# One edge tile in 75 fetched row by row on ScalarE's queue, in the three edge passes of a graph network

## The chip, the cores and the metric

The kernel runs on one core of a Trainium2 chip. A core has a TensorE for matrix products (PE in the profile, its weight loads PEld), VectorE (DVE), ScalarE (ACT), GpSimd (POOL) and SyncE (SP), each with its own queue of instructions, and 16 DMA engines that they share. SP and ACT can issue DMAs at plain or computed addresses; POOL issues the indirect DMAs, whose row numbers lie in a tile. The metric is the device time of one execution in microseconds; before the change it is 34,256.46 us, the median of 10 runs (34,220.72 to 34,300.81).

## The reference

There are 30,000 nodes with 128 features and 960,000 edges, sorted by destination. Layer 0 normalises, applies relu, and runs two relational convolutions over the edges:

```
W   = einsum('rb,bdf->rdf', coeff, basis)        # 32 relations from 8 bases
Hr  = einsum('nd,rdf->nrf', h, W)
agg = segment_sum(Hr[src, etype] * norm, dst)    # + bias
```

Layer 1 is gated. For each of four edge types t it makes tables k, q and v of the nodes, and sums over the edges of type t

```
eta = sigmoid(k[dst] + q[src]);  msg = eta * v[src];  agg = segment_sum(msg, dst)
```

and adds `x @ Ws[t] + b[t]`; the four results are averaged. Both layers are added to x.

## The kernel before

The edges are cut into 7500 tiles of 128 (`TP`), three tiles make a group (`G`), five groups a block (`S`), five blocks a stage (75 tiles, `NTS`, 25 groups, `NGS`), four stages one turn of a hardware loop, and 25 turns a pass. There are three passes over all edges: two of the body in `rel_body` (the convolutions, tables `h0` and `h1`), and one of `gate_body` (table `qvtab`, 256 numbers a row). A turn is written out in full, in order, by hand (`manual_schedule`); an engine executes its own part of that order.

For each tile, `gather` (L117) has POOL issue an indirect DMA that brings 128 rows of the source nodes into SBUF, one edge a partition. In `rel_body`, VectorE makes for each tile a matrix `sb` (L476) from the edge's place in a window of 32 destinations and its coefficients; TensorE multiplies gathered rows and `sb` into the bank `pa` (L481), the three tiles of a group added together; ScalarE copies `pa` into `ab` (L485); and once a block TensorE multiplies `ab` with the bases (`bases_out`, L437). VectorE adds the finished windows to `agg`, which lies in SBUF (L374). The gathered tiles `hg` have 5 buffers, one a group, `sb` has 12, `pa` has 3. In the first pass SyncE loads edge types (`types`, `er`, L397), VectorE makes one-hot rows of them (L405), TensorE turns these into coefficients (L410), and those of the second pass are stored by ScalarE's queue (`keep`, L430) and loaded again in the second pass (`kept`, L435).

In `gate_body`, SyncE loads for each group 128 rows of the key table (`window`, `kw`, L521, 10 buffers, five groups ahead), at an address from a register; TensorE spreads them over the edges into `pk` (L538, 4 banks); VectorE adds the gathered q part of `qv` (L579); ScalarE takes the sigmoid in place (L580); two groups later VectorE multiplies with the v part (L547) and TensorE sums into windows (L549). `qv` has 10 buffers.

Beside the edge work, steps on the nodes are spread over the groups (`beside`): after the first pass's sums the hidden rows `h1`, in the second pass the tables `ktab` and `qvtab` (L655 to L709), in the third the output. Their stores go on ScalarE's queue. Stage loads (`idx` or `qi`, `relc`, `firsts`, `nrm`) go on SyncE's queue a stage ahead. The first destinations of a stage's groups are loaded into registers (`bases`, L360) on VectorE and, in the third pass, SyncE. The compiled program gives the DMAs of SP and ACT eight completion semaphores in turn; a DMA waits until the one eight before it in program order has landed.

Of the kernel before, what the change touches and what calls it, by code (L numbers as in the profile page):

```python
# [9 lines left out]
F32 = mybir.dt.float32  # L10
I32 = mybir.dt.int32
# [10 lines left out]
N = 30000  # L22
# [8 lines left out]
TP = 128  # L31
NT = E // TP
G = 3
# [3 lines left out]
S = 5  # L37
SB = 5
NQ = 4
NS = NQ * SB  # L40
NGS = S * SB
NTS = NGS * G
# [8 lines left out]
LEAD = 3 * VB  # L51
GAP = 8
EPS = 1e-5
CH = 5
PX, KX = 120, 10
IN_RANGE = "destinations are node numbers, below N"


def rows_of(col, n):
# [13 lines left out]
def kernel(  # L73
# [29 lines left out]
    nc = tc.nc  # L103
# [7 lines left out]
    qvtab = nc.dram_tensor("qvtab", (NX * T, 2 * D), F32, kind="Internal").ap()  # L111
    reld = nc.dram_tensor("reld", (TP, NT), F32, kind="Internal").ap()
    kcode = nc.dram_tensor("kcode", (E,), BF16, kind="Internal").ap()
    qidx = nc.dram_tensor("qidx", (TP, NT), I32, kind="Internal").ap()
    ce2 = nc.dram_tensor("ce2", (NI * NS, TP, S * G * B), F32, kind="Internal").ap()

    def gather(to, table, idx):  # L117
        nc.gpsimd.indirect_dma_start(  # L118
            out=to, out_offset=None, in_=table,
            in_offset=bass.IndirectOffsetOnAxis(ap=idx, axis=0))  # L120
# [23 lines left out]
    eps = consts.tile([P, 1], F32, name="eps")  # L144
    nc.vector.memset(eps, EPS)

# [37 lines left out]
    flag = consts.tile([1, 1], I32, name="flag")  # L184
    CT, CG = NT // CH, NGR // CH
    STEPS = N // (PX * KX)
    with tc.tile_pool(name="prep", bufs=2) as prep, tc.tile_pool(name="pre", bufs=4) as pre, \
            tc.tile_pool(name="prep_ps", bufs=1, space=PSUM) as prep_ps:
        lo = prep.tile([TP, CH], F32, name="lo", bufs=1)
        hi = prep.tile([TP, CH], F32, name="hi", bufs=1)  # L190

# [37 lines left out]

        for c in range(CH):  # L230
            edge_chunk(c)
            for i in range(c * STEPS // CH, (c + 1) * STEPS // CH):
                node_chunk(i)
        bad = prep.tile([TP, 2, CH], F32, name="bad", bufs=1)
        nc.vector.tensor_scalar(bad[:, 0, :], lo, 0.0, None, op0=ALU.is_lt)
# [60 lines left out]
    def sorted_path():  # L296
# [5 lines left out]
        with ExitStack() as all_:  # L302
# [57 lines left out]
            def bases(t, engine):  # L360
                _, vals = nc.values_load_multi_w_load_instructions(
                    t[:, :NGS], engines=[engine],
                    min_val=0, max_val=N - 1, skip_runtime_bounds_check_because=IN_RANGE)
                return vals

            def edge_row(row, i, s, n):

                return bass.AP(tensor=row.tensor, offset=(i * NG + s * S) * GE,
                               ap=[[0, n], [GE, S], [1, GE]])
# [6 lines left out]
            def rel_body(table, weights, second):  # L376
# [4 lines left out]

                def body(bas, i, io, pool, ps, cp, iw, ic, beside):
                    stage = {}
                    er, oh, pc, ce, ce_next, ab, po, base = {}, {}, {}, {}, {}, {}, {}, {}

                    def loads(k):
                        stage[k] = [stage_tile(io, "idx", src, I32, i, k),
                                    stage_tile(io, "relc", reld, F32, i, k),
                                    firsts(io, i, k)]
                        if not second:  # L390
                            stage[k].append(
                                stage_tile(io, "nrm", norm, F32, i, k, 4 * TQ - S * G))
# [62 lines left out]
                    for s in range(NS):  # L455
                        k = s // SB
                        if s % SB == 0:
                            if s:
                                tc.stage_boundary()
                            if k + 1 < NQ:  # L460
                                loads(k + 1)
                        if s % SB == 2:
                            leave_stage()
                        idx, relc, start = stage[k][:3]
                        if s + 2 < NS:
                            (kept if second else types)(s + 2)
                        ab[s] = pool.tile([P, B, S, W], F32, name="ab")
                        for g in range(S):
                            t0 = (s % SB * S + g) * G
                            hg = pool.tile([TP, G, D], F32, name="hg", bufs=5)  # L470
                            for j in range(G):
                                gather(hg[:, j, :], table, idx[:, t0 + j:t0 + j + 1])
                            pa = ps.tile([P, B, W], F32, name="pa", bufs=3)
                            for j in range(G):
                                sb = pool.tile([TP, B, W], F32, name="sb", bufs=12)
                                nc.vector.scalar_tensor_tensor(  # L476
                                    sb, iw[:TP].unsqueeze(1).to_broadcast([TP, B, W]),
                                    relc[:, t0 + j:t0 + j + 1],
                                    ce[s][:, g * G + j, :].unsqueeze(2).to_broadcast([TP, B, W]),
                                    op0=ALU.is_equal, op1=ALU.mult)  # L480
                                nc.tensor.matmul(pa.rearrange("p b w -> p (b w)"),  # L481
                                                 lhsT=hg[:, j, :],
                                                 rhs=sb.rearrange("p b w -> p (b w)"),
                                                 start=(j == 0), stop=(j == G - 1))
                            nc.scalar.copy(ab[s][:, :, g, :], pa)  # L485
                            if g == 1 and s:
                                bases_out(s - 1)
                            if g == 2 and not second and s + 1 < NS:
                                coefficients(s + 1)
                            if g == 3 and not second:  # L490
                                keep(s)
                                if s + 2 < NS:
                                    onehot(s + 2)
                            if g == 3 and s > 1:
                                add_windows(po[s - 2], base[(s - 2) // SB], s - 2)
                            if g == 3 and s % SB == 1:
                                base[k] = bases(start, DVE)
                            beside(s * S + g)
# [4 lines left out]

            def gate_body(i, io, pool, ps, cp, iw, ic, beside):
                stage = {}
                kb, oh, kw, sel, pk, qv, po, base, kbase = {}, {}, {}, {}, {}, {}, {}, {}, {}

                def loads(k):
                    stage[k] = [firsts(io, i, k)] + [stage_tile(io, *a, i, k) for a in (
# [25 lines left out]
                def keys(n):  # L535
                    pk[n] = ps.tile([TP, G, D], F32, name="pk", bufs=4)
                    for j in range(G):
                        nc.tensor.matmul(pk[n][:, j, :],  # L538
                                         lhsT=oh[n // S][:, n % S, j * TP:(j + 1) * TP],
                                         rhs=kw[n], start=True, stop=True)  # L540

                def sums(n):
                    s, g = n // S, n % S
                    if g == 0:
                        po[s] = ps.tile([P, S, W], F32, name="po")
                    msg = pool.tile([TP, G, D], F32, name="msg", bufs=3)
                    nc.vector.tensor_mul(msg, pk[n], qv[n][:, :, 1, :])  # L547
                    for j in range(G):
                        nc.tensor.matmul(po[s][:, g, :], lhsT=msg[:, j, :],  # L549
                                         rhs=sel[s][:, g * G + j, :],  # L550
                                         start=(j == 0), stop=(j == G - 1))
# [7 lines left out]
                for n in range(NG):  # L559
                    s, g, k = n // S, n % S, n // NGS  # L560
                    if n % NGS == 0:
                        if n:
                            tc.stage_boundary()
                        if k + 1 < NQ:
                            loads(k + 1)
                    if g == 0 and s % SB == 2:
                        leave_stage()
                    if g == 0 and s + 1 < NS:
                        types(s + 1)
                    if n + S < NG:  # L570
                        window(n + S)
                    qv[n] = pool.tile([TP, G, 2, D], F32, name="qv", bufs=10)
                    t0 = n % NGS * G
                    for j in range(G):
                        gather(qv[n][:, j].rearrange("p a f -> p (a f)"), qvtab,
                               stage[k][1][:, t0 + j:t0 + j + 1])
                    if n + 1 < NG:
                        keys(n + 1)
                    nc.vector.tensor_add(pk[n], pk[n], qv[n][:, :, 0, :])  # L579
                    nc.scalar.activation(pk[n], pk[n], AF.Sigmoid)  # L580
                    if n > 1:
                        sums(n - 2)
                    if g == 1 and s + 1 < NS:
                        onehot(s + 1)
                    if g == 4 and s:
                        add_windows(po[s - 1], base[(s - 1) // SB], s - 1)
                    if g == 4 and s % SB == 0:
                        base[k] = bases(stage[k][0], DVE)
                    beside(n)
# [347 lines left out]
    with tc.If(n_bad == 0) as cmp:  # L937
        sorted_path()
# [63 lines left out]
```

## Time and profile before

| what | value |
|---|---|
| median of 10 runs | 34,256.46 us |
| profiled execution's own time, its span | 34,293.53 us, 34,291.8 us |
| mean granted TensorE clock | 0.677 of full speed |
| busy: PE, PEld, DVE, ACT, POOL | 58%, 49%, 36%, 11%, 62% |
| indirect gathers (L118) | 15,000 of `hg` at 946 ns, 7500 of `qv` at 945 ns |
| gathers of `hg`, of `qv`, first and last start | 196.6 to 22,577.1 us; 22,621.6 to 34,259.3 us |
| DMA queue of POOL (q0) | 840,000 packets, 1967.52 MB |
| DMA queues of SP (q1) and ACT (q10) | 923,347 and 406,197 packets |

The durations are of one profiled execution, whose own time lies within the range of the ten runs. Instructions on registers and semaphores and those that issue DMAs are not counted as busy; a line such as "SPq" or "ACTq" is of such an instruction. In a line of groups, the number behind the bar is the busy time and the mean of one in ns, and behind the second bar stands the engine's idle time just before them and what ended most of it: the instruction that released it, "issue" where the profile shows no wait, "remote" where it knows no releaser. In the timeline each line has its start, its length, engine, line, operation and count, and in brackets the idle time ahead of it. In a list by line or tile the three numbers are the shortest, the median and the longest duration in ns.

### The profile page before, as it was taken

The page shows a single profiled execution, that of the slowest core. Times are in us where ns is not written, and L with a number is a line of the kernel's source. Part 1 is how long each engine was busy: PE and PEld are TensorE (multiplying, and loading weights), DVE is VectorE, ACT ScalarE, POOL GpSimd, SP SyncE. Part 2 cuts the span into 40 slices and gives each one's busy share as a digit, 9 for nine tenths or more (in the row PEclk, how much of TensorE's full clock was granted, in tenths as well). Part 3 has the DMA queues.
Part 4 walks back from the last instruction along what each step waited for, and adds up shares of the span by engine and source line. Part 5 has one row for each costly group of instructions (what it writes and reads, how often), then busy time and mean ns, then how long its engine had stood idle before and what let it go on. Part 6 is the DMA issues. An engine that isn't in the chain of part 4 may idle for free.

```text
span 34291.8 us, 321519 instructions
## 1 busy us (share of the span) xinstructions
PE 19888.5 (58%) x83304; PEld 16933.1 (49%) x83304; DVE 12372.1 (36%) x32695; ACT 3634.5 (11%) x9834; POOL 21303.1 (62%) x22514
## 2 busy tenths in 40 slices
PE   4555555555555566666666666655555555555555
PEld 3444444444444444444444444445555555555555
DVE  3333333333333333333333333333333333333333
ACT  1000000000000011111111111111111111111111
POOL 5666666666666666666666666656666666666665
PEclk8777777777777777777777777765555555555555
DMA  3222222222222222222222222234444444444444
GB/s 98 63 64 63 64 64 64 63 63 63 64 63 63 65 65 66 65 66 65 66 65 66 66 65 66 66 103 123 123 123 121 121 123 124 121 122 122 122 124 118
DMA packets 2171202, 2914.97 MB, mean 85 GB/s; under 512 B 684764, under 2 KB 1617880, under 8 KB 2169544
## 3 DMA queue, kind: packets, MB, share of 16 engines
q0 software_dynamic: 840000, 1967.52, 21.5%
q1 hardware_dynamic: 923347, 651.19, 6.6%
q10 hardware_dynamic: 406197, 276.11, 2.8%
q8 instruction: 802, 13.14, 0.2%
q14 instruction: 856, 7.01, 0.1%
HBM read 2618.79 MB, written 274.16 MB: 84 GB/s over the span
## 4 chain that ended last, share of the span: by engine, by line


## 5 line engine op out<-in xcount | busy, mean ns | idle before, releaser
L118 POOL DMA_INDIRECT hg<-h,idx x15000 | 14187.7, 946 | 8362.6 <-issue 4341.2
L481 PE MATMUL pa<-sb,hg 128*128 128x256 f32 x30000 | 9225.5, 465 | 6161.8 <-issue 3308.5
L481 PEld LDWEIGHTS pa<-sb,hg 128*128 128x128 f32 x30000 | 6900.0, 239 | 7986.1 <-issue 3838.4
L118 POOL DMA_INDIRECT qv<-qvtab,qi x7500 | 7088.4, 945 | 4593.7 <-issue 2256.8
L476 DVE SCALAR_TENSOR_TENSOR sb<-cp,relc,ce 128x256 f32<-128x256 f32 x15000 | 6129.1, 475 | 5245.0 <-remote 4012.1
L549 PE MATMUL po<-sel,msg 128*128 128x32 f32 x15000 | 3450.6, 386 | 4638.6 <-DVE msg L547 3265.6
L549 PEld LDWEIGHTS po<-sel,msg 128*128 128x128 f32 x15000 | 3406.8, 326 | 4937.1 <-DVE msg L547 3443.6
L538 PE MATMUL pk<-kw,oh 128*128 128x128 f32 x15000 | 3956.0, 437 | 307.1 <-DVE oh L525 271.0
L579 DVE TENSOR_TENSOR pk<-pk,qv 128x384 f32<-128x384 f32 x2500 | 1407.2, 563 | 7010.5 <-remote 5459.5
L485 ACT COPY ab<-pa 128x256 f32<-128x256 f32 x5000 | 1807.3, 373 | 19970.0 <-remote 10210.2
L538 PEld LDWEIGHTS pk<-kw,oh 128*128 128x128 f32 x15000 | 3452.1, 330 | 309.8 <-issue 309.8
L440 PE MATMUL po<-ab,bas 128*128 128x160 f32 x16000 | 2483.2, 311 | 371.4 <-ACT ab L485 215.2
L440 PEld LDWEIGHTS po<-ab,bas 128*128 128x128 f32 x16000 | 2406.7, 199 | 480.3 <-ACT ab L485 243.1
L374 DVE TENSOR_TENSOR agg<-agg,po 128x32 f32 x7500 | 1401.9, 187 | 2827.7 <-remote 704.3
L580 ACT ACTIVATE pk<-pk 128x384 f32<-128x384 f32 x2500 | 1186.0, 475 | 9316.8 <-DVE pk L579 5765.0
L676 PE MATMUL bank<-wall,hT 128*120 128x512 f32 x1524 | 1033.9, 801 | 937.7 <-issue 305.0
L547 DVE TENSOR_TENSOR msg<-pk,qv 128x384 f32<-128x384 f32 x2500 | 1368.3, 548 | 108.0 <-remote 95.8
L410 PE MATMUL cp<-coeff,oh 128*128 128x64 f32 x4000 | 689.2, 307 | 937.1 <-issue 800.4
L410 PEld LDWEIGHTS cp<-coeff,oh 128*128 128x128 f32 x4000 | 681.8, 232 | 1003.6 <-issue 905.6
L525 DVE TENSOR_TENSOR oh<-kb,cp 128x1920 f32<-128x1920 bf16 x500 | 1072.4, 2145 | 47.1 <-issue 31.8
L687 DVE TENSOR_TENSOR kt<-bank,ball 120x512 f32<-120x512 f32 x254 | 175.7, 692 | 2211.8 <-remote 788.0
L676 PEld LDWEIGHTS bank<-wall,hT 128*120 128x120 f32 x1524 | 344.4, 244 | 1269.8 <-issue 661.3
(77 smaller groups left out, 3383.1 us busy)
## 6 DMA issues: line engine op xcount, KB each, us to landing
hg<-h,idx POOLq DMA_INDIRECT x15000
kb<-kcode SPq DMA_DIRECT2D x500, 480.0 KB
kw<-ktab SPq DMA_DIRECT2D x2500, 64.0 KB
er<-in_et_row SPq DMA_DIRECT2D x2000, 64.0 KB
qvtab<-qvt ACTq DMA_DIRECT2D x254, 480.0 KB
qv<-qvtab,qi POOLq DMA_INDIRECT x7500
ktab<-kt ACTq DMA_DIRECT2D x254, 240.0 KB
ce<-ce ACTq DMA_DIRECT2D x500, 60.0 KB
```

Of the source, the lines that this page charges most:

```text
L118: nc.gpsimd.indirect_dma_start(out=to, out_offset=None, in_=table, in_offset=bass.IndirectOffsetOnAxis(ap=idx, axis=0))
L374: nc.vector.tensor_add(to, to, po[:, g, :])
L410: nc.tensor.matmul(pc[s][:, c].rearrange("p q l b -> p (q l b)"), lhsT=oh[s][:, c, :], rhs=coeff.rearrange("p q l b -> p (q l b)"), start= ...
L440: nc.tensor.matmul(po[s].rearrange("p s w -> p (s w)"), lhsT=bas[:, b, :], rhs=ab[s][:, b].rearrange("p s w -> p (s w)"), start=(b == 0), ...
L476: nc.vector.scalar_tensor_tensor(sb, iw[:TP].unsqueeze(1).to_broadcast([TP, B, W]), relc[:, t0 + j:t0 + j + 1], ce[s][:, g * G + j, :].uns ...
L481: nc.tensor.matmul(pa.rearrange("p b w -> p (b w)"), lhsT=hg[:, j, :], rhs=sb.rearrange("p b w -> p (b w)"), start=(j == 0), stop=(j == G ...
L485: nc.scalar.copy(ab[s][:, :, g, :], pa)
L538: nc.tensor.matmul(pk[n][:, j, :], lhsT=oh[n // S][:, n % S, j * TP:(j + 1) * TP], rhs=kw[n], start=True, stop=True)
L547: nc.vector.tensor_mul(msg, pk[n], qv[n][:, :, 1, :])
L549: nc.tensor.matmul(po[s][:, g, :], lhsT=msg[:, j, :], rhs=sel[s][:, g * G + j, :], start=(j == 0), stop=(j == G - 1))
L579: nc.vector.tensor_add(pk[n], pk[n], qv[n][:, :, 0, :])
L676: nc.tensor.matmul(bank(a, VB, T * D), lhsT=hT, rhs=wall[:, a].rearrange("p t f -> p (t f)"), start=True, stop=True)
```

## The change

The last tile of each stage is no longer gathered by POOL. Its 128 rows come into a tile of their own, `hx`, by 128 DMAs of one row each on ScalarE's queue. For that the stage's first group loads the tile's 128 row numbers into one partition (`ix`, on SyncE's queue), and after the copy of each of the first 21 groups (in the third pass: after each sigmoid) ScalarE issues the next 6 or 7 rows; ahead of every 16 it loads 16 numbers into registers. The product that used the last part of `hg` uses `hx`. In the third pass VectorE's addition and multiplication are split for a stage's last group, two tiles of `qv` and one of `hx`. This holds for all three passes.

```diff
+XR = 16
+NGX = NGS - 4
...
+            def last_tile(io, pool, table, array, i, k):
+                ix = io.tile([1, TP], I32, name="ix")
+                nc.sync.dma_start(
+                    ix, array[:, ds(i * (NQ * NTS) + (k + 1) * NTS - 1, 1)].rearrange("p o -> o p"))
+                to = pool.tile([TP, table.shape[1]], F32, name="hx")
+                vals = []
+
+                def fetch(n):
+                    for p in range(n * TP // NGX, min((n + 1) * TP // NGX, TP)):
+                        if p % XR == 0:
+                            _, vals[:] = nc.values_load_multi_w_load_instructions(
+                                ix[:, p:p + XR], engines=[mybir.EngineType.Activation], min_val=0,
+                                max_val=table.shape[0] - 1,
+                                skip_runtime_bounds_check_because=IN_RANGE)
+                        nc.scalar.dma_start(to[p:p + 1, :], table[ds(vals[p % XR], 1), :])
+
+                return to, fetch
...
                             hg = pool.tile([TP, G, D], F32, name="hg", bufs=5)
+                            rows = [hg[:, j, :] for j in range(G)]
+                            if t0 == 0:
+                                last[k] = last_tile(io, pool, table, src, i, k)
+                            if t0 + G == NTS:
+                                rows[-1] = last[k][0]
                             for j in range(G):
-                                gather(hg[:, j, :], table, idx[:, t0 + j:t0 + j + 1])
+                                if t0 + j + 1 < NTS:
+                                    gather(rows[j], table, idx[:, t0 + j:t0 + j + 1])
...
-                                                 lhsT=hg[:, j, :],
+                                                 lhsT=rows[j],
...
                             nc.scalar.copy(ab[s][:, :, g, :], pa)
+                            last[k][1](s % SB * S + g)
...
+                def parts(n):
+
+                    if n % NGS + 1 < NGS:
+                        return [(slice(0, G), qv[n])]
+                    hx = last[n // NGS][0].rearrange("p (o a f) -> p o a f", o=1, a=2)
+                    return [(slice(0, G - 1), qv[n][:, :G - 1]), (slice(G - 1, G), hx)]
...
-                    nc.vector.tensor_mul(msg, pk[n], qv[n][:, :, 1, :])
+                    for js, rows in parts(n):
+                        nc.vector.tensor_mul(msg[:, js], pk[n][:, js], rows[:, :, 1, :])
...
+                    if t0 == 0:
+                        last[k] = last_tile(io, pool, qvtab, qidx, i, k)
                     for j in range(G):
-                        gather(qv[n][:, j].rearrange("p a f -> p (a f)"), qvtab,
-                               stage[k][1][:, t0 + j:t0 + j + 1])
+                        if t0 + j + 1 < NTS:
+                            gather(qv[n][:, j].rearrange("p a f -> p (a f)"), qvtab,
+                                   stage[k][1][:, t0 + j:t0 + j + 1])
...
-                    nc.vector.tensor_add(pk[n], pk[n], qv[n][:, :, 0, :])
+                    for js, rows in parts(n):
+                        nc.vector.tensor_add(pk[n][:, js], pk[n][:, js], rows[:, :, 0, :])
                     nc.scalar.activation(pk[n], pk[n], AF.Sigmoid)
+                    last[k][1](n % NGS)
```

More of the change, by code (lines that the diff above doesn't have):

```diff
@@ L53 @@
 EPS = 1e-5
+XR = 16
+NGX = NGS - 4
 CH = 5
 PX, KX = 120, 10
-IN_RANGE = "destinations are node numbers, below N"
+IN_RANGE = "the edges' ends are node numbers, below N"
 def rows_of(col, n):
@@ L383, in body @@
                     stage = {}
-                    er, oh, pc, ce, ce_next, ab, po, base = {}, {}, {}, {}, {}, {}, {}, {}
+                    er, oh, pc, ce, ce_next, ab, po, base, last = {}, {}, {}, {}, {}, {}, {}, {}, {}
                     def loads(k):
@@ L505, in gate_body @@
                 stage = {}
-                kb, oh, kw, sel, pk, qv, po, base, kbase = {}, {}, {}, {}, {}, {}, {}, {}, {}
+                kb, oh, kw, sel, pk, qv, po, base, kbase, last = ({} for _ in range(10))
                 def loads(k):
```

## The prediction

> **What bounds the kernel now.** I read the busy times first, then the costliest groups, then the timeline of some blocks, and last the single instructions that the new work resembles.
>
> ```profile
> span 34291.8 us, 321519 instructions
> PE 19888.5 (58%) x83304; PEld 16933.1 (49%) x83304; DVE 12372.1 (36%) x32695; ACT 3634.5 (11%) x9834; POOL 21303.1 (62%) x22514
> L118 POOL DMA_INDIRECT hg<-h,idx x15000 | 14187.7, 946 | 8362.6 <-issue 4341.2
> L118 POOL DMA_INDIRECT qv<-qvtab,qi x7500 | 7088.4, 945 | 4593.7 <-issue 2256.8
> L485 ACT COPY ab<-pa 128x256 f32<-128x256 f32 x5000 | 1807.3, 373 | 19970.0 <-remote 10210.2
> ```
>
> No engine is full. The gathers come nearest: 14187.7 + 8362.6 + 7088.4 + 4593.7 = 34,232 us, nearly the whole span, or 1.52 us for each of 22,500. The timeline shows that this is not one speed.
>
> ```profile
> 5004.98 0.94 POOL L118 DMA_INDIRECT hg<-h,idx  x1 [0.30 <-issue]
> 5006.23 0.94 POOL L118 DMA_INDIRECT hg<-h,idx  x1 [0.30 <-issue]
> ...
> 5009.80 0.65 ACT L485 COPY ab<-pa 128x256 f32<-128x256 f32 x2 [10.31 <-remote]
> 5010.04 0.94 POOL L118 DMA_INDIRECT hg<-h,idx  x1 [2.87 <-remote]
> 5010.10 4.79 DVE L476 SCALAR_TENSOR_TENSOR sb<-cp,relc,ce 128x256 f32<-128x256 f32 x12 [7.86 <-remote]
> ...
> 5032.03 0.34 DVE L618 TENSOR_SCALAR agg<-bank,b2c 128x120 f32 x1 [14.07 <-PE cp L410]
> 5032.44 0.94 POOL L118 DMA_INDIRECT hg<-h,idx  x1 [3.97 <-PE cp L410]
> ```
>
> Free gathers follow each other at 0.94 + 0.30 = 1.25 us. About once a block of 15, though, VectorE, ScalarE and TensorE all stand still, for 6 to 14 us, and start again together; POOL runs on into its spare `hg` buffers and then stops for 3 to 4 us. Free, 22,500 gathers need 28.1 ms; the standstills make the other 6.1 ms. In the lists by tile `hg` is gathered from 196.6 to 22577.1 us and `qv` from 22621.6 to 34259.3, so a stage of 75 tiles takes 111.9 us in the first two passes and 116.4 in the third, 113.4 on the mean: 4.53 us a group and 22.7 a block, where POOL alone would need 93.8, 3.75 and 18.75.
>
> The nearest rows for the new work are ScalarE's own store at a computed address, SyncE's five loads in a row, SyncE's one-partition load, loads of registers, and ScalarE's first stores:
>
> ```profile
> L430 ACTq FUSED_REGOPS  x500: 52/55/60, 226.3 to 11583.0; - x167
> L430 ACTq MOVE ce<-ce x500: 29/29/35, 226.6 to 11583.1; - x167
> L430 ACTq DMA_DIRECT2D ce<-ce x500: 337/338/389, 226.7 to 11583.2; - x167
> 22623.48 2.68 SPq L521 DMA_DIRECT2D kw<-ktab  x5
> L251 ACTq TENSOR_LOAD <-flag x1: 1278/1278/1278, 185.7 to 185.7; - x1
> L361 DVEq TENSOR_LOAD <-firsts x300: 1841/1846/2699, 242.4 to 34199.4; - x150
> L357 SPq DMA_DIRECT2D firsts<-in_first_st x300: 2/278/722, 194.4 to 34037.4; - x150
> 1.22 6.64 ACTq L152 DMA_DIRECT2D coeff<-in_coeff  x8
> ```
>
> None of these issues counts as busy, so the 11% of ACT hides them.
>
> **The change, part by part.**
> *Removed:* 300 gathers, one a stage. Each gives back 1.25 us where POOL sets the pace (375 us) and at most its share of the whole, 1.52 (457 us).
>
> *Added on ScalarE, a stage:* 128 row fetches, each an address computation, a move and a DMA issue; 8 register loads of 16 indices. They stand after the copies (or sigmoids) of the first 21 of 25 groups, 6.1 rows and 0.38 loads a group.
> A row: the three durations of L430 make 0.055 + 0.029 + 0.338 = 0.42 us, the lower end (with the one-partition 0.278 it would be 0.36, but that is SyncE's). The five loads took 2.68 us, 0.54 each with the steps between; the eight stores 6.64 us, 0.83 each, the upper end. I take 0.50, between 0.42 and 0.54, because L430 is the same engine and instruction kind.
> A load: 1.28 us. VectorE's load of 25 values (1.85) costs no more than its load of the one `flag` (1.91 in the same list), so the count should not matter; 1.85 is the upper end, SyncE's 0.70 the lower.
> A group then holds ScalarE for 6.1 × 0.50 + 0.38 × 1.28 = 3.54 us, beside what it does today: 3405 us busy in 32,900 us of the three passes, 0.47 a group, and about 0.13 of store issues. Sum 4.14 us a group, 20.7 a block. That is over POOL's free 3.75 and close under the present 4.53.
>
> *What covers it.* ScalarE idles about 30 ms (L485's 19,970 us and the sigmoid's 9317), but in large pieces before one copy or sigmoid. A row lies behind its group's copy and ahead of the next one, so in a standstill ScalarE can do one group's rows, 3.54 us, and then waits with the rest. The cover is the three `pa` banks (four `pk`): a late copy delays TensorE's third group on, then VectorE's `sb`, then the release of `hg`, and so POOL.
> I take a standstill at 8 us, between TensorE's 6.0 before L481 at 5010.69 and VectorE's 14.07; 8 − 3.5 = 4.5 us stay uncovered. Block: 20.7 + 4.5 = 25.2 against 22.7, +2.5. In 4.2 of 5 blocks that is +10.5 a stage. If standstills are covered whole, a block is 20.7 and the loss is nothing; with rows at 0.83 it is 30.8 + 4.5, +12.6, or +53 a stage.
>
> *Added on SyncE:* 300 loads of `ix`, 128 words to one partition, behind the stage's other loads and, in the first pass, four `er` loads. The first register load waits for it, and with it the copies behind. SyncE can issue ahead, so nothing is the lower end; the upper is four such issues and a landing, some 6 us by "6.19 us for four `er`" in the timeline. I take 2.
>
> *Added waits:* the compiled program gives all SP and ACT DMAs eight semaphores in turn, and a DMA waits for the eighth before it. Rows now stand between SyncE's loads, so `kw`, `kb`, `er` and `ce` can be fetched about eight DMAs (1.3 groups) ahead of ScalarE instead of several groups. `kw` is used five groups later, `er` three: covered, nothing; if not, `kb`, needed one group after its issue, shows as waits of VectorE's L525, which idles 47 us before it in the whole run today.
> TensorE waits for eight semaphores before the 75th tile, four groups after its last row: nothing. VectorE's two split operations in the third pass, 0.57 us and under, lie beside its idle 64%. The 512 or 1024 bytes of a row are the bytes the gather moved.
>
> *Sum a stage:* +10.5 + 2 − 1.25 = +11.3 us; by 300, +3.4 ms. Against the profiled execution's 34,293.5 us (span 34,291.8) that is 37,680; the median of the ten times is 37 us lower (34,256.5), so I say 37,650.
>
> [...] L430's records hold ScalarE for 0.42 us a DMA, whatever its landing takes. [...]
>
> **Rivals.**
> *ScalarE has room (faster).* For it: 30 ms idle on ScalarE, 0.42 us by its own rows, no record of L430's MOVE over 35 ns, so standstills may not slow ScalarE at all; and 4.14 is still under 4.53. Against it: rows cannot run past the next copy. POOL then gains 300 × 1.25 to 1.52: 33,800 to 33,880. It decides where rows, loads and standstill together stay under 22.7 a block: with 0.42 (18.3 of work) an uncovered remainder under 4.4 us.
> *The standstills grow with the DMAs issued.* POOL's pace without them is the same in all passes, yet a block takes 22.8 us in the first (`er` from 195.2, `ce` of the second from 11,612.9), 21.9 in the second and 23.3 in the third, with 7.1, 2.6 and 7.1 issues of SP and ACT (counted in the DMA list). In one standstill the four `er` issues took 6.19 us. That is 0.2 to 0.3 us a DMA; 129 a stage cost 26 to 39 us, less 1.25: 41,700 to 45,600 us in all. Against it: the passes differ in much else, and a row is 1 descriptor where those are 128.
> *SyncE starves TensorE or VectorE* because it can no longer run ahead: the third pass alone slower, each `kb` late by the 2.68 us of five `kw`: 500 blocks, +1.3 ms, less the 0.4 of the gathers where ScalarE is not yet the bound: 35,200.
> *Nothing moves*, gain and bubbles cancelling: 34,250.
>
> **How the numbers follow.** ScalarE as the bound, 35,000 to 41,000 us: 0.52. Standstills that grow: 0.18. Room: 0.20. SyncE: 0.07. Nothing: 0.03. A measurement of this kernel tells about 0.2%, 70 us, from no change; so faster 0.20, same 0.03, slower 0.77. The range goes from the faster case's 33,800 to 42,800, inside the growing standstills; above stay their upper part and rows of 0.83, some 0.15.
>
> **What would show it.** Right: rows (the new DMA line on ACT) 0.45 to 0.55 us apart inside a group; "issue" or ACT ahead of `pa` and `po` matmuls; POOL's gathers waiting longer although fewer; group time 5 us in groups 0 to 20 and 4.5 after. Wrong, faster: POOL's stops unchanged at 3 to 4 us a block and ACT still idle before L485. Wrong, slower still: FUSED_REGOPS and MOVE on ACT at 0.7 us. The time fails most easily by the standstills: I know that they recur, not what makes them.

## The result, and the profile after

The changed kernel takes 39,058.1 us (median of 8, 38,991.0 to 39,132.9) against 34,256.5 (median of 28): a ratio of 1.1402 [1.1392, 1.1412], 4.8 ms slower. The forecast was 37,650, 3.4 ms slower.

The page of the changed kernel, its busy times and costliest groups:

```profile
span 39049.5 us, 440107 instructions
PE 20885.7 (53%) x83304; PEld 17408.2 (45%) x83304; DVE 12541.7 (32%) x32895; ACT 3659.7 (9%) x9834; POOL 21012.5 (54%) x22214
L120 POOL DMA_INDIRECT hg<-h,idx x14800 | 13993.1, 945 | 12025.7 <-PE pa L509 4967.0
L120 POOL DMA_INDIRECT qv<-qvtab,qi x7400 | 6992.4, 945 | 5974.2 <-DVE msg L584 2745.0
L513 ACT COPY ab<-pa 128x256 f32<-128x256 f32 x5000 | 1843.1, 371 | 17836.2 <-DMA hx<-h 5836.6
```

The busy times have hardly moved, TensorE's most, by 1.0 ms. The gathers' idle time has: 12,025.7 + 5974.2 = 18,000 us, where the kernel before has 8362.6 + 4593.7 = 12,956. That is +5044; with 291 us less of busy gathers it makes up nearly all of the 4758 us between the two spans. The span has 118,588 instructions more, and next to none of them counts as busy.

The single instructions of the row fetches (L384) and of the register loads (L380), with their shortest, median and longest time in ns, and a stretch of ScalarE's timeline (start and length in us):

```profile
L384 ACTq FUSED_REGOPS  x38400: 1/37/1458, 220.9 to 39030.5; - x199
L384 ACTq MOVE hx<-h x25600: 1/29/1637, 221.0 to 26056.1; - x199
L384 ACTq DMA_DIRECT2D hx<-h x25600: 1/234/1411, 222.6 to 26056.2; - x199
L380 ACTq TENSOR_LOAD <-ix x2400: 3/1296/3042, 219.8 to 39022.6; - x185
```

```profile
6001.63 0.37 ACT L513 COPY ab<-pa 128x256 f32<-128x256 f32 x1 [5.19 <-DMA hx<-h]
6001.78 2.23 ACTq L384 DMA_DIRECT2D hx<-h  x6
...
6038.60 2.72 ACTq L384 DMA_DIRECT2D hx<-h  x6
...
6044.66 9.04 ACTq L384 DMA_DIRECT2D hx<-h  x6
6053.79 0.37 ACT L513 COPY ab<-pa 128x256 f32<-128x256 f32 x1 [10.46 <-remote]
6053.94 4.14 ACTq L384 DMA_DIRECT2D hx<-h  x6
```

Six rows take 2.23 us or 9.04, from the start of the first transfer to the end of the last; in the open a row starts 0.40 us after the one before. In the slow bundles even address computations and moves between registers are drawn out, at most to 1458 and 1637 ns; others show 1 ns. So it is not mainly their transfers that the rows wait for; by these times ScalarE's queue itself is held up.

Who waits longest, with total time, times, and the longest:

```profile
ACT pk L621 <- DMA hx<-qvtab: 6112.9, 1158, 40.3
ACT ab L513 <- DMA hx<-h: 5836.6, 1167, 16.1
POOL hg L120 <- PE pa L509: 4967.0, 1198, 13.3
```

ScalarE's copies and sigmoids stand behind rows, and POOL behind TensorE. That is the forecast's mechanism, ScalarE as the bound, and the single instructions of the trace bear it out for the groups with rows. The starts of two successive copies lie 5.54 us apart on the mean where rows follow, in a stage's first 21 groups, and 3.22 in its last four; the sigmoids of the third pass, 5.68 and 2.50. Before the change these were 4.34 and 5.15, and 4.37 and 6.18. So the last four groups catch up, faster than POOL's free 3.75. From the first to the last instruction of each bundle, rows and loads hold ScalarE's queue for 31.2 ms in all, 4.96 us for each of the 6300 groups, where the forecast counted 3.54. What is left to find is why they are so long.

### The profile page after: what moved, and what is told of

Read it like the earlier page. It is cut to its first block, busy times and chain, and to the rows that moved or that the text cites. A ratio compares the mean times of both kernels' runs of the same rounds, so it can differ in the third digit from the quotient of the medians.

```text
span 39049.5 us, 440107 instructions
## 1 busy us (share of the span) xinstructions
PE 20885.7 (53%) x83304; PEld 17408.2 (45%) x83304; DVE 12541.7 (32%) x32895; ACT 3659.7 (9%) x9834; POOL 21012.5 (54%) x22214
## 4 chain that ended last, share of the span: by engine, by line
## 5 line engine op out<-in xcount | busy, mean ns | idle before, releaser
L120 POOL DMA_INDIRECT hg<-h,idx x14800 | 13993.1, 945 | 12025.7 <-PE pa L509 4967.0
L120 POOL DMA_INDIRECT qv<-qvtab,qi x7400 | 6992.4, 945 | 5974.2 <-DVE msg L584 2745.0
L509 PEld LDWEIGHTS pa<-sb,hg 128*128 128x128 f32 x29600 | 6781.1, 239 | 6828.5 <-issue 3570.3
L586 PE MATMUL po<-sel,msg 128*128 128x32 f32 x15000 | 3608.8, 398 | 5326.5 <-DVE msg L584 4643.0
L462 PE MATMUL po<-ab,bas 128*128 128x160 f32 x16000 | 2955.4, 349 | 1663.9 <-ACT ab L513 1190.2
L462 PEld LDWEIGHTS po<-ab,bas 128*128 128x128 f32 x16000 | 2816.7, 230 | 1930.5 <-ACT ab L513 1327.3
L718 PE MATMUL bank<-wall,hT 128*120 128x512 f32 x1524 | 1122.6, 864 | 1945.7 <-ACT hT L714 1356.5
L698 PE MATMUL bank<-ident,xs 128*120 128x128 f32 x254 | 108.6, 429 | 2307.8 <-ACT xs L695 1993.4
L442 DVE TENSOR_TENSOR ce<-cp,nrm 128x128 f32<-128x128 f32 x1000 | 266.2, 284 | 3237.8 <-DMA ce<-ce 2446.3
```

Of the source, the lines that this page charges most:

```text
L120: nc.gpsimd.indirect_dma_start(out=to, out_offset=None, in_=table, in_offset=bass.IndirectOffsetOnAxis(ap=idx, axis=0))
L462: nc.tensor.matmul(po[s].rearrange("p s w -> p (s w)"), lhsT=bas[:, b, :], rhs=ab[s][:, b].rearrange("p s w -> p (s w)"), start=(b == 0), ...
L509: nc.tensor.matmul(pa.rearrange("p b w -> p (b w)"), lhsT=rows[j], rhs=sb.rearrange("p b w -> p (b w)"), start=(j == 0), stop=(j == G - 1))
L586: nc.tensor.matmul(po[s][:, g, :], lhsT=msg[:, j, :], rhs=sel[s][:, g * G + j, :], start=(j == 0), stop=(j == G - 1))
L718: nc.tensor.matmul(bank(a, VB, T * D), lhsT=hT, rhs=wall[:, a].rearrange("p t f -> p (t f)"), start=True, stop=True)
```

## The experiments

Two theories to begin with. A: the rows, at the speed that they have in the open, hold ScalarE, so copies and sigmoids are late. B: the common standstills, in which VectorE, ScalarE and TensorE stop together, grow with what ScalarE and SyncE put through.

The chips differ, so a time is only ever set beside the kernel before on the same chip:

| run | before, us | this, us | ratio [95%] |
|---|---|---|---|
| the change | 34,256.5 | 39,058.1 | 1.1402 [1.1392, 1.1412] |
| e1_one_dma | 34,394.7 | 34,069.0 | 0.9905 [0.9888, 0.9922] |
| e2_rows_on_sp | 34,394.7 | 42,846.5 | 1.2459 [1.2438, 1.2480] |
| e3_fixed_rows | 34,394.7 | 35,250.3 | 1.0249 [1.0232, 1.0266] |
| e5_act_copies | 34,394.7 | 34,627.5 | 1.0068 [1.0051, 1.0085] |
| e6_computed | 28,452.6 | 28,075.2 | 0.9868 [0.9852, 0.9885] |
| e7_fixed_loads | 28,452.6 | 28,121.9 | 0.9885 [0.9869, 0.9902] |
| e4_half_rows | 28,452.6 | 28,082.0 | 0.9870 [0.9854, 0.9887] |
| e8_small_copies | 28,452.6 | 28,075.8 | 0.9868 [0.9852, 0.9885] |
| after_again (the change) | 33,953.7 | 38,619.2 | 1.1374 [1.1355, 1.1393] |
| after_third (the change) | 33,996.3 | 38,551.9 | 1.1344 [1.1325, 1.1363] |
| e6_again | 33,996.3 | 37,567.8 | 1.1049 [1.1030, 1.1067] |
| e8_again | 28,441.7 | 28,062.7 | 0.9866 [0.9850, 0.9883] |

**e1_one_dma: the gather left out, and nothing put through for it**

```diff
-                    for p in range(n * TP // NGX, ...):
-                        if p % XR == 0: ...registers from ix...
-                        nc.scalar.dma_start(to[p:p + 1, :], table[ds(vals[p % XR], 1), :])
+                    if n == 0:
+                        nc.scalar.dma_start(to, table[:TP, :])
```

> The 75th tile comes by one DMA of 128 consecutive table rows on ScalarE's queue (so these edges get the wrong sources; no row numbers, no register loads). This is the change's gain by itself. Theory A (ScalarE is held by the rows, its copies and sigmoids come late) and theory B (the common standstills grow with the number of DMAs issued by SP and ACT) agree: 300 gathers by 1.25 to 1.52 us less, 33,800 to 33,880 us, ratio to before 0.987 to 0.989. If it is not below 0.995, a gather is not worth what the pace says.

0.9905, just above what was expected: 325.7 us, 1.09 for each of 300 gathers, near the forecast's 1.25. What is left out is a gain; the loss is all in what is added.

**e2_rows_on_sp: the same rows and loads on SyncE's queue**

```diff
-  engines=[mybir.EngineType.Activation], ...
-  nc.scalar.dma_start(to[p:p + 1, :], table[ds(vals[p % XR], 1), :])
+  engines=[SP], ...
+  nc.sync.dma_start(to[p:p + 1, :], table[ds(vals[p % XR], 1), :])
```

> The same 128 row DMAs, register loads and places in the program, but on SyncE's queue. Theory A: ScalarE is free again, most of the loss goes; ratio 0.99 to 1.03, what stays being SyncE's own loads coming late. Theory B: as many DMAs and register instructions as in the change, so the loss stays: ratio 1.10 to 1.15.

1.2459, outside both. With ScalarE free of rows it is worse. But SyncE is no empty queue either. Its waits and a stretch of its timeline:

```profile
DVE oh L427 <- DMA er<-in_et_row: 4859.2, 288, 29.6
...
DVE oh L554 <- DMA kb<-kcode: 3972.7, 411, 19.3
```

```profile
8004.86 2.89 SPq L419 DMA_DIRECT2D er<-in_et_row  x4
...
8011.75 7.33 SPq L384 DMA_DIRECT2D hx<-h  x6
...
8025.45 17.31 SPq L384 DMA_DIRECT2D hx<-h  x24
```

VectorE's one-hots now wait 8.8 ms for `er` and `kb`, where before they idled 59 us (L405) and 47 (L525) in all: those loads queue behind rows. The run mixes that with the standstills (6 rows in 7.33 us), so it decides neither theory, only that moving the rows to SyncE does not help.

**e3_fixed_rows: 128 transfers, no address work**

```diff
-  nc.scalar.dma_start(to[p:p + 1, :], table[ds(vals[p % XR], 1), :])
+  nc.scalar.dma_start(to[p:p + 1, :], table[p * 64:p * 64 + 1, :])
```
(with `ix` and the register loads left out)

> 128 row DMAs a stage on ScalarE as in the change, but of fixed rows (wrong sources): no register loads, no address computation, one instruction a row instead of three. Theory A: a row falls from 0.40 us in the open to about 0.25, and 8 loads of 1.3 us go; a group holds ScalarE about 2.1 us; ratio 0.99 to 1.05. Theory B counted by DMAs: unchanged, 1.12 to 1.15; counted by instructions of SP and ACT: two thirds of the added instructions go, 1.03 to 1.06.

1.0249. The transfers alone cost 35,250.3 − 34,069.0 = 1181 us over the single one, a quarter of what the change adds. B in its first form, so much per DMA, falls: it asked for 1.12 to 1.15. By instructions it asked for 1.03 to 1.06, a little more than was measured. The measured ratio also lies within theory A's 0.99 to 1.05.

**e5_act_copies: ScalarE held for as long, without transfers**

```diff
-  nc.scalar.dma_start(to[p:p + 1, :], table[ds(vals[p % XR], 1), :])
+  nc.scalar.copy(filler, ident.unsqueeze(1).to_broadcast([P, G, P]))
```
(128 a stage beside the single transfer of e1)

> As the run with one DMA, and ScalarE does 128 useless copies of 128x384 a stage where the rows stood (0.4 to 0.5 us each, no DMA, no register work). Theory A: ScalarE is held as long as by the rows in the open, about 0.4 to 0.5 us by 6.1 a group: ratio 1.03 to 1.14. Theory B: no DMA is added, so 0.99 to 1.00.

1.0068, outside A's 1.03 to 1.14, and just above B's 0.99 to 1.00. Its group of copies, and the busy time:

```profile
PE 20269.5 (59%) x83304; PEld 17100.0 (49%) x83304; DVE 12421.1 (36%) x32895; ACT 22382.8 (65%) x48234; POOL 21016.3 (61%) x22214
...
L376 ACT COPY filler<-ident x38400: 488/511/546, 216.2 to 34586.1; 128x384 f32<-128x384 f32 x199
```

A copy holds ScalarE for 0.51 us, more than a row in the open (0.40), at the same places, and the loss over e1 is 558 us, not some 5 ms. So ScalarE has room for rows as long as they are in the open. But none of these copies takes over 546 ns, so the run does not tell what rows cost that do hold ScalarE for 4.96 us a group.

**e6_computed, e7_fixed_loads, e4_half_rows, e8_small_copies**

These were to split the rest: the address instructions without the loads (e6), the loads with few address instructions (e7), half of everything (e4), and many short copies with neither (e8).

```diff
e6: +  nc.scalar.dma_start(to[p:p + 1, :], table[ds(i * 64 + p * 64, 1), :])
e7: +  at = vals[XR - 1] if p % XR == XR - 1 else p * 64
    +  nc.scalar.dma_start(to[p:p + 1, :], table[ds(at, 1), :])
e4: +  if n == 0:
    +      nc.scalar.dma_start(to[HALF:, :], table[:TP - HALF, :])
    +  for p in range(n * HALF // NGX, ...):
e8: +  for _ in range(2):
    +      nc.scalar.copy(filler, ident[:, :1])
```

> The 128 row transfers of a stage are issued by ScalarE with an address worked out in registers, but from the loop's variable and the row's number, so that no index tile and no register load is left (wrong sources: the sums are not the reference's). It has the address instructions of the change without its loads. If the address instructions that ScalarE puts through beside the transfers are what costs (38,400 FUSED_REGOPS and 25,600 MOVE in the changed kernel), the ratio to before is 1.10 to 1.14. If it is the 2400 register loads of 1.3 us, with the wait for the index tile, it is 1.02 to 1.05, as with fixed addresses (1.025).

> The index tile and all eight register loads of a stage are back on ScalarE, but only one row in sixteen uses a loaded value; the other 120 have fixed addresses (wrong sources). The mirror of the run with computed addresses. If the loads and the wait for the index tile cost the rest of the change, 1.10 to 1.14; if the address instructions do, 1.03 to 1.05 (8 loads of 1.3 us are 10.4 us a stage of some 115 us, and ScalarE has room for them).

> Rows 0 to 63 of the tile are fetched singly as in the change, rows 64 to 127 by one transfer of fixed rows (wrong sources for those). If the cost goes with the number of instructions that are put through, it is halfway between the single transfer and the change: (0.990 + 1.140) / 2 = 1.065, taken as 1.05 to 1.08. If ScalarE must first run out of room, so that there is a threshold, it is below 1.03.

> The tile comes by a single transfer, and where the rows stood ScalarE makes 256 useless copies of 128x1 a stage (wrong sources): no transfer and no register instruction is added, but 76,800 instructions, two thirds of the 118,000 that the change adds. If the common standstills lengthen with the instructions that an engine completes, whatever they are, at the 0.04 us each that the change shows ((39058 - 34069) us / 118,000), it costs 3.1 ms over the single transfer: ratio 1.07 to 1.09. If only transfers and register instructions do it, 0.99 to 1.02.

All four came out between 0.9868 and 0.9885; of the expectations only e4's "below 1.03" holds that. The reason: on their chip the kernel before takes 28,452.6 us. The forecast had split the 34.2 ms into 28.1 ms of free gathers and 6.1 ms of standstills; here there is little more than the 28.1. So the runs did not answer what they were made for, but they answered another question, whether the rows cost anything where there are hardly any standstills. The rows of e6 on that chip, and ScalarE's timeline:

```profile
span 28066.0 us, 436029 instructions
PE 20892.1 (74%) x83304; PEld 16275.3 (58%) x83304; DVE 12520.8 (45%) x32895; ACT 3725.6 (13%) x9834; POOL 21021.5 (75%) x22214
PEclk8888888888888888888888888875555555555555
L120 POOL DMA_INDIRECT hg<-h,idx x14800 | 13998.8, 946 | 4722.3 <-issue 3837.7
L120 POOL DMA_INDIRECT qv<-qvtab,qi x7400 | 6995.7, 945 | 2302.1 <-issue 1960.2
L373 ACTq FUSED_REGOPS  x38400: 52/55/60, 208.5 to 28038.3; - x199
L373 ACTq MOVE hx<-h x25600: 29/29/44, 208.6 to 18740.6; - x199
...
6000.20 2.32 ACTq L373 DMA_DIRECT2D hx<-h  x6
6007.59 2.32 ACTq L373 DMA_DIRECT2D hx<-h  x6
6011.23 2.33 ACTq L373 DMA_DIRECT2D hx<-h  x6
```

No address computation of a row takes over 60 ns, no move over 44; the bundles of six shown take 2.32 or 2.33 us, others near them up to 2.6; POOL's idle time is mostly "issue", its own step. 128 rows a stage at computed addresses then cost nothing: the kernel gains 377.5 us, 1.26 for each gather left out, and e4 and e8 gain about as much. e7, with `ix` and all 2400 loads of 1.30 us, gives 47 us of it back.

**after_again, after_third and e6_again: back where there are standstills**

> The changed kernel itself, once more, because the four runs with computed addresses, loads beside fixed addresses, half the rows and small copies came from a chip on which the kernel before takes 28,453 us and no common standstill is to be seen, so that they can't be set beside 1.140. If this run falls on such a chip and the common standstills carry the whole loss, the changed kernel is no slower than before there: 0.985 to 1.00 (the gathers left out are worth 0.013, and ScalarE has 6.1 rows of 0.41 us, a third of a 1.3 us load and 0.6 us of its own a group, 3.5 us, against groups some 3.6 us apart). If rows and loads hold ScalarE beyond its room whether there are standstills or not, it is 1.02 to 1.10. If it falls on a chip with standstills (before near 34,300 us), it repeats 1.13 to 1.15.

> The changed kernel beside the run with computed addresses, on one chip. On a chip with standstills (before 33,900 to 34,400 us) 1.13 to 1.15 again. On one without (before near 28,450 us): 0.985 to 1.00 if the whole loss is the standstills', 1.02 to 1.10 if ScalarE has no room for rows and loads.

> The rows at computed addresses without loads, to be set beside the changed kernel on the same chip. On a chip with standstills: 1.10 to 1.14 if the address instructions (or the number of instructions) carry the loss beyond fixed addresses, 1.02 to 1.05 if the register loads and their index tile do. On one without, 0.987 again.

Both repeats of the change fell on chips with standstills and gave 1.1374 and 1.1344. e6_again is e6 unaltered, beside the second of them: 37,567.8 us, 9.5 ms over what the same program takes above. The page and the rows of e6_again:

```profile
span 37631.0 us, 436029 instructions
PE 20618.3 (55%) x83304; PEld 17313.7 (46%) x83304; DVE 12541.6 (33%) x32895; ACT 3664.4 (10%) x9834; POOL 21076.2 (56%) x22214
PEclk8777777777777777777777777775555555555555
L120 POOL DMA_INDIRECT hg<-h,idx x14800 | 14034.7, 948 | 11237.6 <-PE pa L498 4273.8
L120 POOL DMA_INDIRECT qv<-qvtab,qi x7400 | 7014.5, 948 | 5280.0 <-issue 2191.0
L373 ACTq FUSED_REGOPS  x38400: 1/55/1579, 216.9 to 37611.9; - x199
L373 ACTq MOVE hx<-h x25600: 1/29/1617, 217.0 to 25308.8; - x199
...
6005.61 2.32 ACTq L373 DMA_DIRECT2D hx<-h  x6
...
6024.90 5.39 ACTq L373 DMA_DIRECT2D hx<-h  x6
```

Same instruction count, nearly the same busy times, the same median of 55 ns. The granted clock is lower, 0.670 against 0.740 on the mean, in the first two passes (0.73 and 0.76 against 0.83 and 0.88), but nearly equal in the third (0.50 and 0.51), where POOL's `qv` gathers idle 2978 us more all the same; and TensorE's products take no more time here. What changes is the longest time of an address computation, which goes from 60 to 1579 ns, and the gathers' idle time, from 7024 to 16,518 us, which is the 9.5 ms. Stretches of 2 us and more in which TensorE's products, VectorE and ScalarE all stand still add up to 11.1 ms here and to 0.4 there, and the rows hold ScalarE's queue for 4.61 us a group against 2.91. So the loss of the change comes with the standstills: where there are hardly any, its rows are covered.

How it comes with them is less clear. The rows may be drawn out and hold ScalarE, so that copies come late; or each instruction may lengthen the stop of all engines. Between the kernel before and the change, the common stretches grow from 9.4 to 11.8 ms, half of the 4.8; in e3, with as many transfers as the change, they make 8.5, less than the 9.4 of e1 on its chip. By an estimate from the releasers that the trace shows, ScalarE's queue waits for other engines or for landings for some 25 of 34.3 ms before and 5.5 of 39.0 after the change. That speaks for the first reading, at least for a part; no run separates the two.

Within them, e6_again against after_third on one chip puts the loads and `ix` at 38,551.9 − 37,567.8 = 984 us. Against e3 (by ratios, since the chips differ, so less surely) the 76,800 address instructions cost (1.1049 − 1.0249) × 34,000 = 2720 us. Of the two expectations the one of the address instructions, 1.10 to 1.14, holds.

**e8_again: instructions of any kind?**

> 256 useless copies of 128x1 a stage on ScalarE beside the single transfer (wrong sources), on a chip with standstills if this run falls on one. The runs there gave, over the single transfer's 0.9905, for each instruction added: fixed rows (37,280 more) 0.032 us, computed rows (114,082 more) 0.034 us, the change (118,160 more) 0.042 us, the copies of 128x384 (36,350 more) 0.015 us. If the standstills lengthen with every instruction alike, 76,800 at 0.032 to 0.042 us make 2.5 to 3.2 ms: ratio 1.06 to 1.09. If a copy counts for less than a transfer or a register instruction, at 0.015 us 1.2 ms: 1.02 to 1.03. If copies count for nothing and only the time that they hold ScalarE did, 0.99 to 1.01. On a chip without standstills 0.987 again.

0.9866, on a chip without standstills again. It shows that 76,800 copies of 0.19 us are covered there; whether a copy costs in standstills what a register instruction does was not settled. e5's 558 us for 38,400 copies, 0.015 us each, speaks for less.

## Why the prediction was right or wrong

The sign was right, and the time lay in the range. ScalarE's queue did become what holds up the groups with rows, the case on which the point stood, but by the length that rows have in standstills, not by the 0.50 us each of the forecast.

| a stage of 75 tiles | forecast, us | measured with standstills, us | without, us |
|---|---|---|---|
| gather left out | −1.25 | −1.09 (e1) | −1.26 (e6) |
| 128 transfers issued | in +10.5 | +3.94 (e3 − e1) | 0 (e6) |
| 256 address instructions | in +10.5 | +9.07 (e6_again, e3) | 0 (e6) |
| 8 loads and `ix` | in +10.5, and +2 | +3.28 (after_third − e6_again) | +0.16 (e7 − e6) |
| sum | +11.3 | +15.2 | −1.1 |

The measured sum is the 4555.6 us of after_third, 15.2 a stage. The last sum is an estimate by addition; the change itself was not run on a chip without standstills.

- *The gather:* right, from the row of 1.25 us.
- *A row at 0.50 us:* too dear in the open, where rows start 0.40 us apart (0.42 in e6), about the lower end of 0.42 that came from L430. The sign "0.45 to 0.55 us apart" did not come.
- *A load at 1.28 us:* right, median 1.296.
- *"That is over POOL's free 3.75 and close under the present 4.53":* as arithmetic fair, but not the work that was met. At the speed of the open it would have been covered: e5's copies held ScalarE for 0.51 us where a row takes 0.40 and lost 558 us over e1, and the rows of e6, 2.91 us a group, are covered even where groups follow at POOL's free pace. With standstills, rows and loads held it for 4.96 us a group instead of 3.54.
- *The step that failed: "I take a standstill at 8 us", 3.5 of it covered.* It treated a standstill as a gap of fixed length in which ScalarE can do its rows at their usual speed. In fact ScalarE's row instructions are themselves drawn out: six rows take 9.04 us where they took 2.23. The forecast read the opposite from L430, whose MOVE never exceeds 35 ns. Why it does not is open; in the changed kernel the same store's longest MOVE is 712 ns. The profile of before held the sign already, on SyncE's queue:

```profile
L397 SPq FUSED_REGOPS  x2000: 2/66/1620, 195.2 to 11498.9; - x182
L397 SPq MOVE er<-in_et_row x2000: 2/38/1647, 195.6 to 11499.6; - x182
```

- *The rival "standstills grow with the DMAs issued":* near the cause, in the wrong unit. Per DMA at 0.2 to 0.3 us it gave 41,700 and more; e3 shows 0.03 us a transfer. Two thirds of the instructions of a row are not DMAs. Per instruction the loss is 0.032 us for transfers (1181 us / 37,280) and 0.035 for register instructions (2720 / 76,800). The sign to look for was on record, address computations and moves at 0.7 us, and it came for a part of them: 7% take over 0.5 us, while the medians stay at 37 and 29 ns.
- *The rival "ScalarE has room":* true on chips without standstills, by e4, e6 and e7.
- *"Group time 5 us in groups 0 to 20 and 4.5 after":* the right way and further apart, 5.5 to 5.7 and 3.2 to 2.5.
- *"SyncE starves the others":* not seen as forecast, in the third pass alone; but e2 shows its mechanism, 8.8 ms of waits, once the rows stand in SyncE's own queue. The eight semaphores stand in the records of the kernel before: eight successive DMAs of SP and ACT carry eight different ones in 7438 of 8499 stretches, and of the 8426 DMAs that use one again 8399 came after their engine had waited for it. In the changed kernel SyncE's loads of `kw` (L550) waited 523.7 us for rows to land, 221 times, and those of `kept` (L457) 2344.5 us, 108 times.
- *"POOL's gathers waiting longer although fewer":* right, +5.0 ms, behind `pa`, as the chain was told.

Why the point was 1.4 ms too low: a row's length in the open too high and its length in standstills too low, which partly cancelled. That the range held owes something to luck.

Open stays what makes the standstills and why some chips have hardly any. It is not the program or its traffic alone, for e6 is the same in both. Each chip of the experiments was met on one occasion only, so whether it is the chip or the occasion is open too. What draws short register instructions out, of which in e6_again one took 1 ns and another 1579, is not shown either. Every run was recorded, with 436,029 instructions in both runs of e6, so no run tells whether the recording has a part in it.

## What to carry to other kernels

Before putting a number on a stop that all engines share, ask whether the new instructions run through it at their usual speed: look at the longest, not only the median, time of instructions that wait for nothing, such as moves between registers, on every queue that has them. Here three cheap queue instructions in place of one row of a gather, 118,000 instructions in all, cost 4.8 ms with their engine counted as 9% busy, though its queue was held most of the time; the rows cost nothing where that longest time stays at 60 ns. And set every variant beside the old kernel on the same chip, for the same program took 28.1 ms on one and 37.6 on another.

## What the runs showed of the hardware

- The kernel before takes 28,442 to 28,453 us on two chips where the variants' traces show hardly any standstills (0.4 ms in e6_computed), and 33,954 to 34,395 where they occur (9.4 ms in the profile of before); 300 gathers fewer are worth 1.3% on the former and 0.95% on the latter.
- In the open, one-row transfers at computed addresses follow each other on ScalarE's queue at 0.40 to 0.42 us, fixed ones at 0.30; a load of 16 registers takes 1.30.
- Where standstills occur, an instruction that ScalarE's queue puts through for a row cost 0.032 to 0.035 us of the whole on the mean, though the engine counts as 9 to 11% busy; a copy of 0.51 us cost 0.015.
